# Queries and keys into even rows of the stripes by DMA from SBUF, and another order of the first batch

## The chip, the cores and the metric

The kernel runs on one core of a Trainium2 chip. The metric is the device time of one execution in microseconds (us), the median of several runs. Matrix products run on PE (TensorE; PEld is its weight load), reductions and elementwise work on DVE (VectorE), ACT (ScalarE) and POOL (GpSimd); SP (SyncE) issues nearly all DMAs, in the order of the program. An engine works through its own instructions in order, and a wait holds everything behind it on that engine.

## The reference

Eight sequences of 512 tokens with 256 channels, all in f32, go through four residual stages, each after a layer norm without gain:

```python
def attn_a(x, ...):                       # 16 heads of 16
    q = x @ Wq + bq
    kv = (x @ Wkv_down + bkv_down) @ Wkv_up + bkv_up      # 64 wide in between
    k, v = split(kv per head)
    q, k = rope(q), rope(k)
    att = q @ k.T / 4 + log_sparse + log(decay + 1e-9)    # depend on i - j alone
    out = softmax(att) @ v
    out = out + 0.2 * sigmoid(q @ mean(k).T) * mean(v)
    return out @ Wo + bo

def attn_b(x, ...):                       # one head, causal decay 0.96875, no softmax
    return ((x @ Wq.T + bq) @ (x @ Wk.T + bk).T * D) @ (x @ Wv.T)

x = x + attn_a(layernorm(x))
x = x + relu(layernorm(x) @ W1 + b1) @ W2 + b2
x = x + attn_b(layernorm(x))
x = x + relu(layernorm(x) @ W1 + b1) @ W2 + b2            # the same weights again
```

## The kernel before

The batch b is the outer index. In attention a, heads lie in stripes of 32 partitions, four heads to a group g, four groups to a batch: `qT[b % 2]` and `kT[b % 2]` are `[128, 4, 512]`, and head h of a group has rows 32h to 32h+31. In the kernel before, its 16 dimensions are rows 0 to 15 of the stripe. Row 16 of qT takes minus the row maximum (against a row of ones in kT), so that the product t comes out shifted. The rest of qT's stripe is zero and the rest of kT's is one.

One step of the main loop makes one score item: `s` (two heads, 128 queries by 512 keys, `score_item`), whose maximum DVE takes into `mr` (`reduce_item`). Eight items make a group. `shift(i)` turns the maxima, negates them on ACT and sends them by a DMA into qT (`neg`). Ten steps (`LAG`) after its `s`, the transposed product `t` is made (`prob_item`), ACT takes the exponential, DVE or POOL multiply with the decay `dec_a` (`soft_item`), and two steps later PE multiplies with the values (`pv_item`). The `s` items share two PSUM double banks with the later `t` items (`ps_sc`); the first `t` items and all other products share three banks (`ps_m`, `misc`).

All other work is cut into units (`Unit`), which stand in chains: front of a batch (layer norm `ln_units`, then `latent`, keys, queries, `values`, `gate`, `mean_v`, `through_wo`) and the rest of a batch (`wo_unit`, the two FFNs, attention b). A planner in Python (`step`, `issue`, and the loop at the end) goes through the steps with a model of the engines' clocks and puts units between steps where credit for PE time is left. `keep_in_program_order` pins the order that comes out.

A front makes queries and keys in half units: for e = 0, 1 (the two halves of a head's rotation) one product of PE, and two products of DVE with the tables of cosine and sine (`rc`, `rs`, six buffers of the tag `rot`). `turn(j)` sums them on POOL, writes the two results to a DRAM tile (`dk` or `dq`, by `[head, dimension, token]`), and reads this back into the stripes, four reads, one for each h:

```python
                move(d[:, e * HH : (e + 1) * HH, :], o)
            src = d.rearrange("(g s) r t -> s r g t", s=4)
            to = (qT, kT)[j][b % 2]
            for h in range(4):
                move(to[h * 32 : h * 32 + HD], src[h])
```

From the third batch on, another DMA puts zeros into the maxima's rows (`zero_rows`). `mean_k` and `gate` take the summed tiles for the gated memory; `mean_v` and `through_wo` make its other side (`mem`).

The first batch is written out by hand ahead of the loop: memsets of kT0 and qT0 on DVE, then statistics and norms, the bias products (`biases`, 32 products of one column), the weights' regrouping on ACT (`regroup`), transposes, `memory_buffers` (POOL memsets, small DMAs), then the first eight units of the front (latent, k0, k1, turn, mean_k, q0, q1, turn), then `late_loads` (dec_a, the second batch's x, wo, w1, w2, wvu, dec_b), `plain` and `product` (the combined weight of attention b's scores), values, gate and `mean_v`, `product_biases`, and the second pair of buffers on POOL (`buffers(1, gps)`). `through_wo` of the first batch waits in a chain for step 10.

Of the kernel before, what the change touches and what calls it, by code (L numbers as in the profile page):

```python
# [15 lines left out]
P = 128  # L16
B, T, D = 8, 512, 256
NH, HD = 16, 16
HH = 8
# [16 lines left out]
def tile_kernel(  # L36
# [44 lines left out]
    dr = ctx.enter_context(tc.tile_pool(name="dr", bufs=1, space=bass.MemoryType.DRAM))  # L81
# [8 lines left out]
    def move(to, src):  # L90
        tc.keep_in_program_order(nc.sync.dma_start(to, src))
# [11 lines left out]
    def keep(shape, name):  # L103
        return const.tile(shape, F32, tag=name, name=name)
# [26 lines left out]

    qT = [keep([P, NG, T], f"qT{i}") for i in range(2)]
# [7 lines left out]
    dq = [dr.tile([NH, HD, T], F32, tag=f"dq{i}", name=f"dq{i}") for i in range(2)]  # L140
    dk = [dr.tile([NH, HD, T], F32, tag=f"dk{i}", name=f"dk{i}") for i in range(2)]
# [11 lines left out]
    def buffers(i, eng):  # L153
        eng.memset(kT[i], 1.0)
        eng.memset(qT[i], 0.0)
        gps.memset(vaug[i], 1.0)

    def head_mask():
        dve.reduce_sum(hmask, ident.rearrange("p (h d) -> p h d", d=HH), axis=AX.X)
        gps.tensor_scalar(hmask, hmask, 0.5 / T, None, ALU.mult)  # L160
        gps.memset(kmean, 0.0)

    def memory_buffers():
        for i in range(2):
            gps.memset(gates[i], 0.0)
            move(gates[i][NH : NH + 1, :], rope[HD : HD + 1, 0, :])
            gps.memset(mem[i], 0.0)
        gps.memset(bo_row, 0.0)
        move(bo_row[NH : NH + 1, :], rows[D : 2 * D].unsqueeze(0))
        move(bvc, rows[0:D].rearrange("(c p) -> p c", p=P))  # L170
        gps.memset(vmean, 0.0)
        gps.memset(vmask, 0.0)
        gps.memset(vmask[:, :, NH : NH + 1], 1.0)
        for c in range(NC):
            dve.reduce_sum(
                vmask[:, c, c * HH : (c + 1) * HH], ident.rearrange("p (h d) -> p h d", d=HD), axis=AX.X
            )
        gps.tensor_scalar(bvc, bvc, 0.1, None, ALU.mult)

    late = {}  # L180

    def late_loads():
        late["dec_a"] = resident(decay_a, "dec_a")
        xs[1] = load_x(1)

        for g in range(NG):
            at_row = (g % 2) * 4 * HD
            move(wo_sb[at_row : at_row + 4 * HD, g // 2, :], wo.rearrange("(h d) g n -> h d g n", d=32)[:, :HD, g, :])
        late["w1"] = resident(w1, "w1_sb")
        late["w2"] = resident(w2, "w2_sb")  # L190

        move(wvu[:, :, :D], wb[:, :, 2, :])
        late["dec_b"] = resident(decay_b, "dec_b")
# [12 lines left out]

    wq_sb = keep([P, NC, 2, P], "wq_sb")
    wk_sb = keep([LAT, 2, P], "wk_sb")
    def regroup():
        for e in range(2):  # L210
            half_of = slice(e * HH, (e + 1) * HH)
            act.copy(wk_sb[:, e, :].rearrange("p (h d) -> p h d", d=HH), wk_in[:, :, half_of])
        for e in range(2):
            half_of = slice(e * HH, (e + 1) * HH)
            for c in range(NC):
                act.copy(wq_sb[:, c, e, :].rearrange("p (h d) -> p h d", d=HH), wq_in[:, c, :, half_of])
# [4 lines left out]
    def biases():  # L221
        pick = keep([P, 2, 32], "pick")
        for e in range(2):
            act.copy(
                pick[:, e, :].rearrange("p (s d) -> p s d", d=HH),
                ident.rearrange("p (s d) -> p s d", d=32)[:, :, e * HH : (e + 1) * HH],
            )
        ps = misc("qk_bias")
        for g in range(NG):
            for j, v in enumerate((V_BQ, V_BK)):  # L230
                for e in range(2):
                    mm(ps[g * 32 : g * 32 + 32, 2 * j + e : 2 * j + e + 1], pick[:, e, :], vec[:, v + g : v + g + 1])
        act.copy(qk_bias.rearrange("p j e -> p (j e)"), ps[:, :4])
# [12 lines left out]

    def plain(j):
        ps = misc(f"wr{j}")
        for o in range(NC):
            for c in range(NC):  # L250
                flip(ps[:, o * D + c * P : o * D + (c + 1) * P], wqk_in[:, c, j, o * P : (o + 1) * P])
        wr[j] = rs.tile([P, NC, D], F32, tag="xr", bufs=3, name=f"wr{j}")
        act.copy(wr[j].rearrange("p o d -> p (o d)"), ps)
# [83 lines left out]
    def front1(b):  # L337
        def latent():
            ps = misc(f"lat_{b}")
            for c in range(NC):  # L340
                mm(ps[:LAT, :], wd_sb[:, c, :], xT_a[b]["xT"][:, c, :], c == 0, c == NC - 1)
            lt = fr.tile([LAT, T], F32, tag="lat", name=f"lat_{b}")
            lsum[b] = fr.tile([LAT, 1], F32, tag="lsum", name=f"lsum_{b}")
            act.activation(lt, ps[:LAT, :], AF.Identity, bias=vec[:LAT, V_BD : V_BD + 1], accum_out=lsum[b])
            lat_a[b] = lt
# [15 lines left out]
        def mean_v():  # L361
            ps = misc(f"mv_{b}")
            for c in range(NC):
                mm(ps[:, c : c + 1], wv_sb[:, c * P : (c + 1) * P], lsum[b])
            m = fr.tile([P, NC], F32, tag="mv_a", name=f"mv_a_{b}")
            dve.scalar_tensor_tensor(m, ps[:, :NC], 0.1 / T, bvc, ALU.mult, ALU.add)
            for c in range(NC):
                gps.tensor_scalar(vmean[:, c, : NH + 1], vmask[:, c, :], m[:, c : c + 1], None, ALU.mult)
# [9 lines left out]
        u = {"lat": Unit(latent, 1720, (("ACT", 700),), after=[h0[2], h1[2]])}  # L378
# [11 lines left out]
    def front2(b, u1):  # L390
        rot = {}
        cos, nsin = rope_sb[:, 0, :], rope_sb[:, 1, :]

        def half_unit(j, e):
            ps = misc(f"{'qk'[j]}{e}_{b}")
            if j == 0:
                for c in range(NC):
                    mm(ps, wq_sb[:, c, e, :], xT_a[b]["xT"][:, c, :], c == 0, c == NC - 1)
            else:
                mm(ps, wk_sb[:, e, :], lat_a[b])  # L400
            for n, table in (("c", cos), ("s", nsin)):
                t = fr.tile([P, T], F32, tag="rot", bufs=6, name=f"r{n}{j}{e}_{b}")
                dve.scalar_tensor_tensor(t, ps, qk_bias[:, j, e : e + 1], table, ALU.add, ALU.mult)
                rot[n, e] = t

        def turn(j):

            d = (dq, dk)[j][b % 2]
            for e in range(2):
                o = rot["c", e]  # L410
                if e == 0:
                    gps.tensor_add(o, o, rot["s", 1])
                else:
                    gps.tensor_sub(o, o, rot["s", 0])
                move(d[:, e * HH : (e + 1) * HH, :], o)
            src = d.rearrange("(g s) r t -> s r g t", s=4)
            to = (qT, kT)[j][b % 2]
            for h in range(4):
                move(to[h * 32 : h * 32 + HD], src[h])
            if j == 0:  # L420
                if b > 1:
                    move(to[HD:P:32], zero_rows)
                rot["q"] = rot["c", 0], rot["c", 1]

        def mean_k():
            m = fr.tile([P, 2], F32, tag="mk", name=f"mk_{b}")
            for e in range(2):
                unused = fr.tile([P, T], F32, tag="unused", name=f"unused{e}_{b}")
                act.activation(unused, rot["c", e], AF.Identity, accum_out=m[:, e : e + 1])
                gps.tensor_scalar(kmean[:, e, :NH], hmask, m[:, e : e + 1], None, ALU.mult)  # L430

        def gate():
            ps = misc(f"ga_{b}")
            for e in range(2):
                mm(ps, kmean[:, e, :], rot["q"][e], e == 0, e == 1)
            act.activation(gates[b % 2][:NH, :], ps[:NH, :], AF.Tanh)
# [9 lines left out]
        ga = Unit(gate, 1720, (("ACT", 600),), after=[km, qt], needs=(("wo", b - 2),))  # L446
        return [lat] + k + [kt, km] + q + [qt, u1["v", 0], u1["v", 1], ga, u1["mv"], u1["me"]]
# [23 lines left out]
    def shift(i):  # L471
# [5 lines left out]
        act.dma_start(qT[b % 2][HD:P:32, g, :], neg)  # L477
# [237 lines left out]
    order0 = front2(0, front[0][1])  # L715
    (n0, n1), u0 = (front[0][0][:3], front[0][0][3:]), front[0][1]
    buffers(0, dve)
    head_mask()
    n0[0].fn(), n1[0].fn()
    biases()  # L720
    regroup()
    n0[1].fn(), n1[1].fn()
    n0[2].fn(), n1[2].fn()
    memory_buffers()
    for u in order0[:8]:
        u.fn()
    late_loads()
    plain(0), plain(1)
    for u in order0[8:12]:
        u.fn()  # L730
    product(), product_biases()
    buffers(1, gps)


# [127 lines left out]
    for u in front[0][0] + order0[:12]:  # L862
        u.done = 0
    order0[12].step = 10
    chains = [order0[12:], setup]
# [168 lines left out]
```

## Time and profile before

| what | us |
|---|---|
| median of 3 runs | 1354.7 |
| lowest, highest | 1354.05, 1356.53 |
| the profiled execution's own time | 1355.33 |
| its span in the profile | 1353.5 |
| PE busy in the span | 1278.4 (94%) |
| DVE, ACT, POOL busy | 805.8, 450.8, 408.3 |
| first score product `s` starts | 39.31 |
| first `t` product starts | 65.37 |

The profile is of one execution. Its times count from the start of the span. An entry of a timeline gives start, length, engine, line, operation, tile written, tiles read, shapes and the number of instructions merged into it, and in brackets how long the engine stood idle before and what ended that. L198, L201, L69 and L91 are the helpers `mm`, `flip`, `Engine` and `move`, so one goes by the tiles' names. A product in f32 appears as two matmul records. "PEclk" is the granted TensorE clock, as a share of full speed in the windows and in tenths in the page's row.

### The profile page before, as it was taken

What the parts mean: (1) busy time and instruction counts of PE and PEld (TensorE: products, weight loads), DVE (VectorE), ACT (ScalarE), POOL (GpSimd) and SP (SyncE); (2) the same over time, 40 slices, a digit from 0 to 9 for tenths busy, and PEclk for the clock granted to TensorE, in tenths of its full rate; (3) what the DMA queues carried; (4) which work ended last, traced back from release to release, by engine and by line L of the source; (5) the groups of instructions that cost most, each with busy time, mean ns of one, the idle gap of its engine ahead of it and who ended that gap; (6) DMA issues with size and microseconds to landing.
All of it is one profiled execution on the core that took longest, in us unless ns stands there. A gap on an engine that the chain in (4) does not pass through costs nothing. (4 is left out here: it accounts for less than half of the span.)

```text
span 1353.5 us, 15551 instructions
## 1 busy us (share of the span) xinstructions
PE 1278.4 (94%) x6116; PEld 632.2 (47%) x6116; DVE 805.8 (60%) x1323; ACT 450.8 (33%) x646; POOL 408.3 (30%) x461
## 2 busy tenths in 40 slices
PE   7889998999899998999999999999999999999989
PEld 3323233535354553545544454535444554455665
DVE  4577976678656686546765667646755484433120
ACT  2034434342434324333343323342343233331201
POOL 4165443233422323223331414213321232222010
PEclk9689989999999999999999999999999999999999
DMA  4440040003000210004000300003000000000000
GB/s 122 134 79 1 1 79 1 1 16 64 1 1 1 63 33 1 0 5 91 1 1 1 68 28 1 1 1 79 1 1 0 17 1 1 1 16 1 0 16 16
DMA packets 22159, 32.09 MB, mean 24 GB/s; under 512 B 2987, under 2 KB 12652, under 8 KB 21806
## 3 DMA queue, kind: packets, MB, share of 16 engines
q1 hardware_dynamic: 21446, 30.83, 10.2%
q8 instruction: 48, 0.79, 0.3%
q10 hardware_dynamic: 640, 0.26, 0.1%
q14 instruction: 25, 0.20, 0.0%
HBM read 18.24 MB, written 12.58 MB: 23 GB/s over the span
## 5 line engine op out<-in xcount | busy, mean ns | idle before, releaser
L69 DVE TENSOR_REDUCE mr<-s 128x2 f32<-128x1024 f32 x256 | 312.4, 1221 | 274.9 <-PE t L198 264.5
L69 ACT ACTIVATE p<-t 128x1024 f32<-128x1024 f32 (+1 forms) x290 | 264.0, 924 | 554.4 <-PE t L198 496.1
L69 POOL TENSOR_TENSOR p<-p,dec_a 128x512 f32<-128x512 f32 x182 | 233.1, 1302 | 490.0 <-ACT p L69 435.6
L198 PE MATMUL s<-kT,qT 32*128 32x512 f32 x1024 | 297.6, 664 | 40.3 <-DVE mr L69 36.5
L198 PE MATMUL t<-qT,kT 32*128 32x512 f32 x1024 | 297.0, 647 | 4.8 <-DVE mr L69 2.5
L69 DVE TENSOR_TENSOR p<-p,dec_a 128x512 f32<-128x512 f32 x330 | 230.1, 738 | 21.5 <-ACT p L69 21.3
L198 PE MATMUL x<-w_sb,h_x 128*128 128x256 f32 x1024 | 233.1, 383 | 0.0
L198 PEld LDWEIGHTS x<-w_sb,h_x 128*128 128x128 f32 x1024 | 190.7, 190 | 52.5 <-issue 27.6
L198 PEld LDWEIGHTS s<-kT,qT 32*128 32x128 f32 x1024 | 81.1, 189 | 208.1 <-DVE mr L69 85.2
L198 PE MATMUL pv<-p,va 128*32 128x512 f32 x1024 | 152.2, 614 | 3.7 <-DVE p L69 3.1
L69 ACT ACTIVATE h_x<-hx,vec 128x512 f32<-128x512 f32 x128 | 88.0, 688 | 156.3 <-PE hx L198 156.3
L198 PE MATMUL hx<-xT_g,w_sb 128*128 128x512 f32 x256 | 122.1, 622 | 0.7 <-ACT xT_g L69 0.7
L198 PE MATMUL hx<-xT_f,w_sb 128*128 128x512 f32 x256 | 119.0, 604 | 0.0
L69 DVE TENSOR_TENSOR x<-x,x 128x256 f32<-128x256 f32 x64 | 27.1, 424 | 153.9 <-PE x L198 153.8
L198 PEld LDWEIGHTS t<-qT,kT 32*128 32x128 f32 x1024 | 80.4, 184 | 22.0 <-issue 9.1
L198 PEld LDWEIGHTS hx<-xT_g,w_sb 128*128 128x128 f32 x256 | 48.0, 196 | 67.7 <-issue 59.8
L198 PEld LDWEIGHTS hx<-xT_f,w_sb 128*128 128x128 f32 x256 | 46.2, 192 | 57.5 <-issue 54.3
L198 PEld LDWEIGHTS pv<-p,va 128*32 128x32 f32 x1024 | 23.6, 108 | 78.2 <-issue 35.4
L69 POOL TENSOR_TENSOR x<-x,row 128x256 f32<-128x256 f32 x64 | 47.7, 765 | 38.4 <-DVE xn_g L69 20.4
L69 POOL TENSOR_TENSOR rc<-rc,rs 128x512 f32<-128x512 f32 x32 | 42.6, 1354 | 10.9 <-DVE rs L69 10.9
L198 PE MATMUL bs<-xT_r,ret 128*128 128x512 f32 (+3 forms) x128 | 38.3, 442 | 0.4 <-DVE mv_a L69 0.4
L198 PE MATMUL bo<-ret 128*128 128x256 f32 x160 | 36.7, 382 | 0.0
(130 smaller groups left out, 1034.5 us busy)
## 6 DMA issues: line engine op xcount, KB each, us to landing
dk<-rc SPq DMA_DIRECT2D x16, 256.0 KB
kT<-dk SPq DMA_DIRECT2D x32, 128.0 KB
dq<-rc SPq DMA_DIRECT2D x16, 256.0 KB
qT<-dq SPq DMA_DIRECT2D x32, 128.0 KB
out_dram<-x SPq DMA_DIRECT2D x32, 128.0 KB
x<-in_x_dram SPq DMA_DIRECT2D x7, 512.0 KB
w_sb<-in_w_dram SPq DMA_DIRECT2D x2, 1024.0 KB
x<-in_x_dram SPq DMA_DIRECT2D x2, 256.0 KB
```

Source lines behind the costliest of these rows:

```text
L69: ins = f(*a, **k)
L198: tc.keep_in_program_order(nc.tensor.matmul(o, lhsT=l, rhs=r, start=start, stop=stop))
```

## The change

- The two DRAM tiles are gone. `stripes(j, g, e)` sends 32 partitions of a summed tile (group g, half e, 2 KB in each) straight into the stripes of qT or kT: half e = 0 goes to rows 0, 4, 8, ... and e = 1 to rows 2, 6, 10, ... So the dimensions lie in the even rows, and the maxima's row is now row 1 of the stripe. A batch has 16 such DMAs in place of 4 writes and 8 reads.
- The first batch gets another order. PE starts with 14 products of the identity with itself (`warm`), whose result nobody reads. The latent of the first batch is made in two halves of 256 tokens, each after its transposes, so that `lsum` has two columns and `mean_v` twice the products. Regrouping is split. Memsets of kT1, qT1 and va1 come earlier, and qT0's comes after the norms. q0 comes ahead of the keys, q1 after them, with its two products in a tile of the tag `p`; the sums of q1 and q0 run on DVE.
- SP gets x_1, dec_a, the gates' rows and bvc ahead of the stripes; the 16 stripes then go group by group; the other late loads follow.
- values, `plain` and `product` stand after the stripes' issue and ahead of the loop; gate, `product_biases`, `mean_v` and `through_wo` (now from step 4) go into the loop as a chain. `wr` lies in the buffer of the tag `x1`.

```diff
-    dq = [dr.tile([NH, HD, T], F32, tag=f"dq{i}", name=f"dq{i}") for i in range(2)]
-    dk = [dr.tile([NH, HD, T], F32, tag=f"dk{i}", name=f"dk{i}") for i in range(2)]
...
+    def loads_before_scores():
+        xs[1] = load_x(1)
+        late["dec_a"] = resident(decay_a, "dec_a")
+        for i in range(2):
+            move(gates[i][NH : NH + 1, :], rope[HD : HD + 1, 0, :])
+        move(bvc, rows[0:D].rearrange("(c p) -> p c", p=P))
+
     def late_loads():
-        late["dec_a"] = resident(decay_a, "dec_a")
-        xs[1] = load_x(1)
+        move(bo_row[NH : NH + 1, :], rows[D : 2 * D].unsqueeze(0))
...
+    def warm(n):
+        ps = misc("warm")
+        for j in range(n):
+            mm(ps[:, j % 4 * P : (j % 4 + 1) * P], ident, ident)
...
-        def latent():
-            ps = misc(f"lat_{b}")
+        def latent(part=0, parts=1):
+            if part == 0:
+                lat_a[b] = fr.tile([LAT, T], F32, tag="lat", name=f"lat_{b}")
+                lsum[b] = fr.tile([LAT, parts], F32, tag="lsum", bufs=1, name=f"lsum_{b}")
+            ps = misc(f"lat_{b}_{part}")
+            n = T // parts
+            cols = slice(part * n, (part + 1) * n)
...
-        def half_unit(j, e):
+        def half_unit(j, e, order="cs"):
...
+                if b == 0 and (j, e) == (0, 1):
+                    if not spare:
+                        spare["t"] = at.tile([P, 2, T], F32, tag="p", bufs=4, name="rq1_0")
+                    t = spare["t"][:, "cs".index(n), :]
+                else:
+                    t = fr.tile([P, T], F32, tag="rot", bufs=6, name=f"r{n}{j}{e}_{b}")
...
+        def rotate(j, e, eng):
+            o = rot["c", j, e]
+            if e == 0:
+                eng.tensor_add(o, o, rot["s", j, 1])
+            else:
+                eng.tensor_sub(o, o, rot["s", j, 0])
+            rot[j, e] = o
+
+        def stripes(j, g, e):
+            move((qT, kT)[j][b % 2][2 * e : P : 4, g, :], rot[j, e][g * 32 : g * 32 + 32, :])
+
         def turn(j):
-            d = (dq, dk)[j][b % 2]
             for e in range(2):
...
-                move(d[:, e * HH : (e + 1) * HH, :], o)
-            src = d.rearrange("(g s) r t -> s r g t", s=4)
-            to = (qT, kT)[j][b % 2]
-            for h in range(4):
-                move(to[h * 32 : h * 32 + HD], src[h])
-            if j == 0:
-                if b > 1:
-                    move(to[HD:P:32], zero_rows)
-                rot["q"] = rot["c", 0], rot["c", 1]
+                rotate(j, e, gps)
+                for g in range(NG):
+                    stripes(j, g, e)
+            if j == 0 and b > 1:
+                move(qT[b % 2][1:P:32], zero_rows)
...
-        act.dma_start(qT[b % 2][HD:P:32, g, :], neg)
+        act.dma_start(qT[b % 2][1:P:32, g, :], neg)
...
-    buffers(0, dve)
-    head_mask()
+    dve.memset(kT[0], 1.0)
+    gps.memset(vaug[0], 1.0)
+    memory_buffers()
+    picks()
+    warm(14)
+    regroup_k()
     n0[0].fn(), n1[0].fn()
+    n0[1].fn(), n1[1].fn()
+    n0[2].fn()
     biases()
-    regroup()
-    n0[1].fn(), n1[1].fn()
-    n0[2].fn(), n1[2].fn()
-    memory_buffers()
-    for u in order0[:8]:
-        u.fn()
+    regroup_q(0)
+    latent(0, 2)
+    masks()
+    dve.memset(qT[0], 0.0)
+    gps.memset(kT[1], 1.0)
+    gps.memset(qT[1], 0.0)
+    gps.memset(vaug[1], 1.0)
+    loads_before_scores()
+    n1[2].fn()
+    latent(1, 2)
+    regroup_q(1)
+    half_unit(0, 0)
+    half_unit(1, 0), half_unit(1, 1, "sc")
+    rotate(1, 0, gps), rotate(1, 1, gps)
+    half_unit(0, 1, "sc")
+    rotate(0, 1, dve), rotate(0, 0, dve)
+
+    for g in range(NG):
+        for j, e in ((1, 0), (1, 1), (0, 1), (0, 0)):
+            stripes(j, g, e)
     late_loads()
-    plain(0), plain(1)
-    for u in order0[8:12]:
-        u.fn()
-    product(), product_biases()
-    buffers(1, gps)
+    order0[1].fn(), order0[2].fn()
+    plain(0), plain(1), product()
+    gps.tensor_scalar(bvc, bvc, 0.1, None, ALU.mult)
+    order0[0].fn()
...
-    for u in front[0][0] + order0[:12]:
+    km0, _, _, ga0, mv0, me0 = order0
+    for u in front[0][0] + [front[0][1]["lat"], km0]:
         u.done = 0
-    order0[12].step = 10
-    chains = [order0[12:], setup]
+    ga0.after = []
+    me0.step = 4
+    chains = [[ga0, Unit(product_biases, 2400, (("DVE", 500),)), mv0, me0], setup]
```

## The prediction

> **What bounds the kernel now.** I read the page first, then windows over the first 110 us, then the timelines of PE, SP and DVE there, then the waits.
>
> ```profile
> span 1353.5 us, 15551 instructions
> PE 1278.4 (94%) x6116; PEld 632.2 (47%) x6116; DVE 805.8 (60%) x1323; ACT 450.8 (33%) x646; POOL 408.3 (30%) x461
> PEclk9689989999999999999999999999999999999999
> ```
>
> PE is busy 94% of the span, so work taken off other engines in the middle is worth little. What stands out is the second and third digit of the clock row. Finer windows (columns: stretch, length, busy PE, PEld, DVE, ACT, POOL, granted clock, DMA share, GB/s):
>
> ```profile
> 34.00:37.00 3.00, 2.29 (x21) 2.20 (x19) 1.40 (x4) 0.00 (x0) 3.00 (x3) 1.00 0.07 24
> 37.00:39.30 2.30, 0.00 (x0) 0.02 (x1) 0.85 (x1) 0.00 (x0) 0.82 (x1) 0.85 0.96 160
> 45.00:50.00 5.00, 5.00 (x14) 1.51 (x12) 4.05 (x7) 0.00 (x0) 0.95 (x2) 0.50 1.02 280
> 50.00:55.00 5.00, 5.00 (x16) 1.89 (x16) 4.60 (x7) 0.56 (x1) 0.00 (x0) 0.50 0.57 224
> 65.00:70.00 5.00, 5.00 (x23) 1.83 (x23) 3.47 (x5) 2.30 (x5) 2.49 (x2) 1.00 0.00 0
> ```
>
> PE stands from 36.3 to 39.3 and the clock falls to 0.50 (the 1-us window 38:39 reads 0.81, so at 38.6). It returns in the window 62:64 (0.87, so at 62.5). Now the PE timeline:
>
> ```profile
> 12.32 3.67 PE L198 MATMUL lat<-xT_a,wd_sb 128*64 128x512 f32 x4 [0.68 <-ACT xT_a L69]
> 16.86 3.78 PE L198 MATMUL k<-lat,wk_sb 64*128 64x512 f32 x4 [0.87 <-ACT lat L69]
> 20.56 5.87 PE L198 MATMUL q<-xT_a,wq_sb 128*128 128x512 f32 x8
> 39.31 14.04 PE L198 MATMUL s<-kT,qT 32*128 32x512 f32 x28 [3.02 <-DMA qT<-dq]
> 63.50 1.93 PE L198 MATMUL lat<-xT_a,wd_sb 128*64 128x512 f32 x4 [0.68 <-ACT xT_a L69]
> 65.37 0.70 PE L198 MATMUL t<-qT,kT 32*128 32x512 f32 x2
> 66.43 1.98 PE L198 MATMUL k<-lat,wk_sb 64*128 64x512 f32 x4
> ```
>
> The same lat and k products take 3.67 and 3.78 in the first batch and 1.93 and 1.98 in the second. So PE also ran at half speed up to about 25 us, though the clock row says 1.00 there. The first seven score steps take 14.04 us, 2.0 each. Why the scores start so late is in SP's timeline:
>
> ```profile
> 23.46 1.77 SPq L91 DMA_DIRECT2D dk<-rc  x2
> 27.68 1.75 SPq L91 DMA_DIRECT2D kT<-dk  x4
> 29.53 1.55 SPq L91 DMA_DIRECT2D dq<-rc  x2
> 36.13 1.72 SPq L91 DMA_DIRECT2D qT<-dq  x4
> ```
>
> Queries leave for DRAM at 29.5 and are read back only at 36.1. In the waits of PE this DMA appears once (3.0 us, one time): later batches never wait for it.
>
> **The change part by part.** My marker is the first t product, at 65.4 us. Behind it the same steps are planned, and PE stays the limit. So I sum up to the marker, against this execution (span 1353.5, time 1355.33; the median 1354.7 is 0.6 below it).
>
> *Front, at full PE speed.* 14 products of ident run from about 1.4 us, when ident is ready: 28 records. A 128-column record at half speed is about 0.21 (0.85, the half-speed pace of 512 columns, divided by four), so at most 6 us, until 7.4. They delay nothing: x_0 is summed to 512 KB by 3.8 us, and transposes began at 7.75. Dropping qT's memset (1.76) and hmask (0.23) from ahead of the statistics lets these start at about 3.8 instead of 5.18. On POOL the moved memsets (2.5 us at 8.2, plus kmean 0.3) now stand ahead of ve_a; they end at about 5.1, when ve_a could have started at 4.8, so 0.3 lost. First norm at 6.15 (was 7.29); the second one took 2.37 beside those memsets and should take 0.73.
>
> Then: transposes 6.6 to 7.3; xT copy 0.59 beside 32 bias products (1.1); lat half 8.4 to 9.4; second transposes to 9.9; ACT's lat and copy to 10.7; lat half to 11.7; q0 (four of eight records at 0.48) to 13.7; k0, k1 to 15.6; q1 to 17.5. DVE makes 8 rotation products (0.66 apart) from 13.8 to 19.1 and two sums until 20.5. POOL makes k's sums (2.49) from about 17.2. ACT's regroup_k waits for wk_in (there by 6.06) and regroup_q for wq_in (there at 8.16, wanted at 8.6): hidden; a later wq_in would hold lat, queued behind it on ACT, one for one. The memsets of kT1, qT1, va1 (4.7 us on POOL) go to about 8 to 13, ahead of k's sums at 17: free.
>
> *Stripes.* A new DMA, SBUF to SBUF, 32 rows of 2 KB. The trace has no such row. From below: neg, 8 KB SBUF to SBUF, is issued in 0.54. From above: qT<-dq, 128 KB, landed about 2.7 after its issue on a full queue. I take 0.42 to issue (kT<-dk's) and 2.5 to land; the four of group 0 are out at 20.9 and landed by 23.5 (bounds 22.5 and 25). The other twelve issue until 26 and are wanted one group per 8 steps.
>
> The Trainium skill, "DMA: Bandwidth & Descriptors", section "Rules for kernel authors", speaks against this: many small transfers should be coalesced, since under 64 KB overhead is most of the cost; its fixed part is about 2 us. Were the 16 to follow each other at that price, group 1 would land at 18 + 8 x 2.1 = 35, still before its step 8 (about 40). By the rule or by the 0.42, the sum is the same.
>
> *Filling the wait.* v (2.0), plain (1.0), product (2.0), already there, run from 17.5; with bank waits for DVE's va (1.62 after the sums) they end at about 24.5. That, not the DMA, starts the scores: 24.5, against 39.3. Some twenty handoffs at under 0.1 us add 1.5: 26.
>
> *Scores to marker.* It took 26.1. At full speed PE needs 10 steps x 1.05, transposes 0.9, mx 0.3, me 1.1, lat 1.9: 14.7. DVE needs 10 x 1.23, layer norm 3.3: 15.6. Moved in: gate 2.0, product_biases 2.4, mean_v with a second column 1.1, and DVE's 1.5 (wvu's row took 1.32 beside POOL). PE 20.2, DVE 17.1; they partly wait for each other through two score banks, so 22. Marker at 48: 17.4 saved.
>
> Here a rule and the trace differ. The skill's "TensorE: Matmul & The Clock Gate", "Part 1", says one busy window of about 3.4 us brings full speed back and one idle window takes it. The changes I can place (38.6, 62.5, 93.2, 103.5, 171.8) are indeed whole multiples of 3.41 apart. But score products alone, with PE shown busy 5.00 of 5, did not bring it back for 23.9 us. By the rule the half-speed stretch would cost some 2 us in scores and the gain be about 12; by the trace it costs what I counted.
>
> *Loads.* x_1, dec_a, gates' rows and bvc (6 issues, some 2.2 us of SP) move ahead of the stripes, into 7 to 9 us, and lengthen the stream of loads from 12.2 to about 15.3; all that the front needs stands ahead of them. wo, now behind the 16 stripes, lands at about 31, wanted by me at about 33; without that cover PE stands 1 to 3 us. w1, w2, wvu, dec_b are wanted far later.
>
> *Later batches.* Per batch SP issues 16 stripes (6.7 us) instead of 4 at 0.55 and 8 at 0.42 (5.6), without its waits for dk and dq. Nothing behind them on SP (x two batches on, outputs) is near: kT and qT of batch 1 landed by 99 and its scores start at about 134. I count zero. The order of units behind the marker may shift by a few steps; half-speed stretches such as 93.2 to 103.5 (worth some 4 us) may come or go: plus or minus 5.
>
> **The rivals.**
> 1. *Clock stays half in part* (27%). For: between 7 and 12 PE holds only short pieces, and the window before 93.2, with 1.1 us of work, was enough to lose the clock; scores alone did not regain it. Against: gate, me, transposes and lat are mixed in. Scores at 33, or 26 plus 30 us: marker 55 to 60, gain 5 to 10: about 1347.
> 2. *More comes free* (10%): the front as summed without slack, and the stall at 90.7 to 93.0 goes too: gain 25, 1329.
> 3. *Stripes are slow in every batch* (4%), the other side. All four of one group read the same 32 partitions. q's eight start at 90 and scores want them at 134: it decides from 5.6 us apiece, one after another. At 6 each, a batch waits 4 us and the lost clock costs 4 more: seven times 8 less 17 gives 1394. Against: 128 KB reads were issued 0.42 apart.
> 4. *Given back* (4%): a new order of units loses as much behind the marker as was won: 1354. That the change does not do what it says I exclude: the order is pinned by hand.
>
> **How the numbers follow.** Likeliest (55%): 1355.3 - 17.4 - 0.6 = 1337. Range 1327 to 1350: rival 2 below, rival 1 above, with the 5 us of order; outside are rivals 3, 4 and the edges. Faster by over 0.2% (2.7 us, about what this measurement can tell from no change) in the likeliest, 1 and 2: 0.92; same 0.04 (rival 4); slower 0.04 (rival 3).
>
> **What would show it.** lat and k at about half of 3.67 and 3.78; first s near 26 without a wait for DMA; no 0.50 between 30 and 55; first t near 48; stripes issued about 0.42 apart; tail unchanged. Wrong, if lat halves take 1.8 each, if the clock reads 0.50 in the scores, or if s of batch 1 waits for DMA.

## The result, and the profile after

The changed kernel takes 1343.06 us (median of 4 runs, 1340.52 to 1343.37) against 1355.15 for the kernel before on the same chip: a ratio of 0.9906 [0.9889, 0.9923]. So it is faster by about 12 us. The forecast was 1337, with a gain of 17.4. The result lies inside the forecast's range, 1327 to 1350, on the side of its first rival.

The profiled execution took 1343.3. The page of the changed kernel (its span, the busy times, the clock row):

```profile
span 1341.5 us, 15714 instructions
PE 1274.7 (95%) x6152; PEld 634.4 (47%) x6152; DVE 804.2 (60%) x1325; ACT 450.8 (34%) x648; POOL 405.3 (30%) x459
PEclk9689999999999999999999999999999999998999
```

PE's busy time fell by 3.7 us only, for a span that is 12.0 shorter. That does not make the rest time in which PE stood: the busy time now holds the 5.2 us of `warm`, which fill time in which PE stood before. Without them PE's work is 8.9 us shorter, and only the other 3.1 of the 12.0 are time in which PE stood. The second digit of the clock row is still 6, so a half-speed stretch is still there. The page's DMA traffic fell from 32.09 MB to 23.70 MB with the trips through DRAM gone.

PE's timeline of the changed kernel:

```profile
1.34 5.17 PE L193 MATMUL warm<-ident 128*128 128x128 f32 x28 [1.34 <-POOL ident masks.py:199]
7.94 1.08 PE L193 MATMUL lat<-xT_a,wd_sb 128*64 128x256 f32 x4
...
11.10 1.08 PE L193 MATMUL lat<-xT_a,wd_sb 128*64 128x256 f32 x4 [1.50 <-ACT xT_a L69]
12.10 1.98 PE L193 MATMUL q<-xT_a,wq_sb 128*128 128x512 f32 x4
14.02 1.98 PE L193 MATMUL k<-lat,wk_sb 64*128 64x512 f32 x4
...
24.35 1.13 PE L193 MATMUL s<-kT,qT 32*128 32x512 f32 x4
25.41 1.12 PE L193 MATMUL ga<-rc,kmean 128*128 128x512 f32 x2
27.23 1.84 PE L193 MATMUL bb<-vec,wr 128*128 128x1 f32 x16
28.93 0.59 PE L193 MATMUL bb<-both,ones 128*128 128x1 f32 x4
29.45 1.13 PE L193 MATMUL s<-kT,qT 32*128 32x512 f32 x4
30.50 1.05 PE L193 MATMUL mv<-lsum,wv_sb 64*128 64x1 f32 x8
...
34.00 2.08 PE L193 MATMUL s<-kT,qT 32*128 32x512 f32 x4 [0.49 <-DVE mr L69]
...
37.50 1.19 PE L193 MATMUL me<-wo_sb,vmean 128*128 128x256 f32 x2 [0.27 <-DMA wo_sb<-in_wo_dram]
...
48.81 1.22 PE L193 MATMUL t<-qT,kT 32*128 32x512 f32 x2
...
54.76 1.98 PE L193 MATMUL k<-lat,wk_sb 64*128 64x512 f32 x4
```

The front runs at full speed: the two lat halves sum to 2.16 where lat took 3.67, and k takes 1.98 where it took 3.78. The first s starts at 24.35 with no wait in brackets (39.31 before, behind a wait of 3.02 for qT). Up to 31 four s records take 1.13. At 34.00 four take 2.08: the clock has gone. It is back by 54.76, where k takes 1.98. The windows show the same (columns: stretch, length, busy PE, PEld, DVE, ACT, POOL, granted clock, DMA share, GB/s):

```profile
26.00:29.00 3.00, 3.00 (x21) 2.28 (x19) 0.82 (x2) 0.59 (x1) 0.00 (x0) 1.00 0.40 106
29.00:32.40 3.40, 3.40 (x23) 2.29 (x24) 2.11 (x5) 0.00 (x0) 0.00 (x0) 1.00 0.30 78
32.40:36.00 3.60, 3.11 (x10) 0.50 (x4) 2.68 (x6) 0.00 (x0) 1.62 (x4) 0.50 0.42 136
46.06:49.48 3.42, 3.42 (x12) 1.42 (x14) 2.32 (x4) 0.63 (x2) 0.00 (x0) 0.50 0.01 2
50.00:55.00 5.00, 5.00 (x21) 1.30 (x14) 1.36 (x2) 1.95 (x5) 2.49 (x2) 0.71 0.01 3
```

The clock is at half speed from 32.4 to 52.9. That is 20.5 us, six times 3.41; before it was seven times 3.41 (38.6 to 62.5). Two lines deserve notice. In the second, the 3.40 us just before the loss, PE is shown busy for all 3.40. In the fourth, PE is busy for all of one such stretch of 3.42, and the clock still does not come back at its end.

The lead of the changed kernel over the one before, taken as the difference of the starts of the same instruction:

| instruction | before | after | lead |
|---|---|---|---|
| first s | 39.31 | 24.35 | 15.0 |
| first t | 65.37 | 48.81 | 16.6 |
| k of the second batch | 66.43 | 54.76 | 11.7 |
| end of span | 1353.5 | 1341.5 | 12.0 |

The order around the marker changed, so the starts need care. Before, lat of the second batch stands ahead of the first t; after, it stands behind (50.82, 2.94 us long), so the first t flatters. k is too harsh: after, one step more (an s and a t, 48.81 to 50.82, so 2.0 us) stands ahead of it. Either way, with lat added to the first t or the step taken off k, the lead for equal work is about 13.7. Behind k it moves between 10.7 and 14.9 (read at the products mx, which turn the score maxima, group by group), and ends at 12.0. So of the 15.0 won at the first s, 1.3 were lost up to the marker and 1.7 behind it. The forecast had counted on 4.1 more between the first s and the marker (13.3 to 17.4); that did not come.

### The profile page after: what moved, and what is told of

Same layout as the page of the kernel before. It is cut to its first block, busy times and chain, and to the rows that moved or that the text cites. A ratio compares the mean times of both kernels' runs of the same rounds, so it can differ in the third digit from the quotient of the medians.

```text
span 1341.5 us, 15714 instructions
## 1 busy us (share of the span) xinstructions
PE 1274.7 (95%) x6152; PEld 634.4 (47%) x6152; DVE 804.2 (60%) x1325; ACT 450.8 (34%) x648; POOL 405.3 (30%) x459
## 2 busy tenths in 40 slices
DMA packets 18576, 23.70 MB, mean 18 GB/s; under 512 B 3500, under 2 KB 13165, under 8 KB 18223
## 5 line engine op out<-in xcount | busy, mean ns | idle before, releaser
L193 PE MATMUL s<-kT,qT 32*128 32x512 f32 x1024 | 293.1, 660 | 38.6 <-DVE mr L69 37.8
L193 PE MATMUL hx<-xT_f,w_sb 128*128 128x512 f32 x256 | 121.9, 617 | 0.0
L69 POOL TENSOR_TENSOR rc<-rc,rs 128x512 f32<-128x512 f32 x30 | 39.6, 1340 | 5.0 <-DVE rs L69 5.0
```

Source lines behind the costliest of these rows:

```text
L69: ins = f(*a, **k)
L193: tc.keep_in_program_order(nc.tensor.matmul(o, lhsT=l, rhs=r, start=start, stop=stop))
```

## The experiments

Two theories were set against each other. One: the score stage is slow because the clock falls, and the clock falls with what TensorE's array has to do, not with how long PE is shown busy. The other: the stage is held by something else (two score banks that wait for DVE, a late wo), and the clock only follows. In all kernels here that carry an added "fill" product, its result is overwritten by the score product that follows; "warm" products have no reader. No output changes by them. Ratios are against the kernel before; a lead is a lead over it in the profiled executions, and these are single ones. Where the work ahead of k differs between two that are compared, the text says so.

**Fill products beside the scores** (on top of the change):

```diff
+            if s < LAG:
+                mms.append((ps[:, 0, :256], ident, rope_sb[:, 0, :256]))
```

> The changed kernel with one more product in each of the first ten score steps (identity times 256 columns of the rope table, written where the step's own score product then starts anew, so nothing of the result changes). Theory A: the score stage of the changed kernel loses about 8 us because score products alone are too little activity for the clock, which falls to 0.50 at 32.4; the fill keeps it at 1.00 up to the first t product, each fill costs 0.43 us, and k of the second batch starts at 48 to 50 instead of 54.8; about 1337 us. Rival B: the stage is bound by waits (two score banks, DVE's maxima, wo's DMA) and the clock costs nothing there; then ten fills come on top, k starts at 57 to 59, about 1347 us.

1348.41 (20 runs, 1340.25 to 1356.92), ratio 0.9965 [0.9947, 0.9983]: worse than the change alone. The clock was lost at 29.7, before the fills had had a chance. PE's timeline and a window of this kernel:

```profile
26.92 1.84 PE L193 MATMUL bb<-vec,wr 128*128 128x1 f32 x16
...
42.00:46.00 4.00, 4.00 (x12) 2.04 (x10) 2.28 (x4) 0.00 (x0) 0.00 (x0) 0.50 0.04 18
```

The 3.41 us ahead of 29.7 hold mostly `bb`, the one-column products of product_biases (1.84, then 0.58). PE had no gap in them. Then fills and scores ran at half speed until 46.8. So the fills did not hold the clock in this execution, which speaks against the first theory as it was stated; but it was one-column products that lost it, and a fill costs 0.6 at full speed and 1.22 at half.

**The front's warm products taken out** (on top of the change):

```diff
-    warm(14)
```

> The changed kernel without the 14 products of the identity at the start. If these set PE's speed in the front: lat halves take 1.8 instead of 1.08, q and k 3.7 instead of 1.98, the first score starts at 30 to 32 instead of 24.4, and the time is about 1349 us. Rival: PE comes up to speed by itself or the front is bound by x, ACT and DVE; first score at 25 to 26, time within 1.5 us of the changed kernel's 1343.

1346.36, ratio 0.9936 [0.9918, 0.9954]. PE's timeline of this kernel:

```profile
8.66 1.97 PE L193 MATMUL lat<-xT_a,wd_sb 128*64 128x256 f32 x4
...
14.24 3.53 PE L193 MATMUL q<-xT_a,wq_sb 128*128 128x512 f32 x4
```

Without them the lat halves take 1.97 in place of 1.08 and q 3.53 in place of 1.98; the first s starts at 28.04, so `warm` is worth 3.7 us there and 2.6 at k (57.40). Its score stage was at half speed for three windows (34.5 to 44.7), not six. The two intervals of the whole time overlap, so how much of this survives is not settled.

**The stripes alone** (the kernel before, its order kept, the two DRAM tiles replaced by the 16 stripes):

```diff
-                move(d[:, e * HH : (e + 1) * HH, :], o)
...
-                move(to[h * 32 : h * 32 + HD], src[h])
+                for g in range(NG):
+                    stripes(j, g, e)
```

> The kernel before with the stripes alone (no DRAM tiles, even rows, maxima in row 1), first batch in its old order. Expected: stripes of group 0 land by about 34, so the first score starts when PE is through with product_biases, at 36.3 instead of 39.3; PE does not stand, so the clock holds for one or two windows of 3.4 us and then falls in the score stage: 1350 to 1352 us. Rival: the stripes also pay in every later batch (a wait for DRAM that the profile does not show), 1340 to 1345; other rival: 16 small DMAs are slower in later batches, above 1355.

1352.13, ratio 0.9984 [0.9967, 1.0]. PE's timeline and two windows of this kernel:

```profile
34.68 1.14 PE L195 MATMUL s<-kT,qT 32*128 32x512 f32 x8
...
34.00:37.00 3.00, 1.82 (x15) 0.98 (x14) 2.18 (x3) 0.00 (x0) 2.29 (x2) 0.99 0.73 223
37.00:42.00 5.00, 4.01 (x10) 1.51 (x12) 4.15 (x8) 0.00 (x0) 0.95 (x2) 0.50 0.92 248
```

The wait for qT is gone and the first s comes 4.6 us earlier, yet the clock falls at 36.95 and stays down for 23.9 us, exactly as long as before. The stand of 3 us was not needed to lose it; a wait of 1.31 us for DVE stood in the window ahead of the loss. What was won at the first s is what is left at the end (lead 4.7 at k, 4.1 at the end of the profiled run; 2.5 in the medians).

**The new order alone** (the changed kernel, with queries and keys through the DRAM tiles):

```diff
-    for g in range(NG):
-        for j, e in ((1, 0), (1, 1), (0, 1), (0, 0)):
-            stripes(j, g, e)
+    for j, e in ((1, 0), (1, 1), (0, 1), (0, 0)):
+        leave(j, e)
+    back(1), back(0)
```

> The changed kernel's order of the first batch with queries and keys still going through DRAM tiles (rows 0 to 15 of the stripes, maxima in row 16, as before). Expected: the round trip of about 8.8 us from the last sum (30.5 to 39.3 in the kernel before) puts the first score at 29 to 31; PE stands from 24.4, the clock falls to 0.50 there and returns only with the first t products; about 1349 to 1351 us. Rival: values, plain and product hide the round trip, first score at 25, 1343 us.

1354.31, ratio 0.9992 [0.9978, 1.0006]: no difference. PE's timeline and a window of this kernel:

```profile
30.97 3.12 PE L197 MATMUL s<-kT,qT 32*128 32x512 f32 x4 [7.13 <-DMA qT<-dq]
...
24.00:28.00 4.00, 0.00 (x0) 0.00 (x0) 0.57 (x1) 0.00 (x0) 0.00 (x0) 0.74 0.70 126
```

All that the new order wins in the front PE spends waiting, 7.13 us, for the trip through DRAM. The clock falls in that wait, at 25.9, and stays down for nine windows, to 56.6; the gate, bias and mean products moved into this stage run at half speed too. The stripes alone bring about 2.5 us, the order alone nothing that can be told, both together 12. The two parts need each other: the order ends sooner only if the keys and queries arrive, and their arrival counts only if PE has got that far.

**product_biases out of the score stage:**

```diff
-    me0.step = 4
-    chains = [[ga0, Unit(product_biases, 2400, (("DVE", 500),)), mv0, me0], setup]
+    pb = Unit(product_biases, 2400, (("DVE", 500),), step=LAG + 1)
+    chains = [[ga0, pb, mv0, me0], setup]
```

> The changed kernel with product_biases, mean_v and through_wo of the first batch held until score step 11, when t products run too; gate stays. Theory A (28 products of one column in the score stage leave PE nearly without activity for a window of the clock): the clock holds 1.00 from the front to the t products; s, gate, transposes and lat up to k of the second batch take about 23 us from 24.4, k starts at 47 to 49 instead of 54.8, and the time is about 1337 us. Rival B (score products alone, two of them at a time on 32 rows each, are too little activity): the clock still falls, at 33 to 37, k starts at 53 to 55, 1342 to 1344 us.

> The same with one product of the identity with 256 columns of the rope table in each of the first ten score steps, overwritten by the step's own score product. Theory A: the clock held anyway, the fills add up to 10 x 0.43 us of PE, of which some hides beside DVE's maxima; k at 49 to 52, 1338 to 1341 us. Rival B: the fills are what holds the clock; k at 49 to 52 where the kernel without them has 53 to 55, so 3 us faster than that one.

The second one has the fills besides. In the chain, mean_v and through_wo stand behind product_biases and move with it. Without fills: 1348.63, ratio 0.9951 [0.9936, 0.9965]. With fills: 1346.74, 0.994 [0.9922, 0.9957]. PE's timeline and a window of the one without fills, then a line of PE's timeline and three windows of the one with:

```profile
34.04 3.20 PE L193 MATMUL s<-kT,qT 32*128 32x512 f32 x8 [0.74 <-DVE mr L69]
...
32.00:36.00 4.00, 3.20 (x10) 1.30 (x12) 3.11 (x6) 0.00 (x0) 0.94 (x2) 0.62 0.28 74
```

```profile
49.01 1.02 PE L193 MATMUL bb<-both,ones 128*128 128x1 f32 x4 [1.49 <-POOL ones L69]
...
36.00:42.00 6.00, 6.00 (x27) 2.49 (x25) 5.17 (x9) 0.82 (x2) 0.94 (x2) 1.00 0.84 345
44.00:48.00 4.00, 3.52 (x25) 2.46 (x24) 1.86 (x3) 1.67 (x3) 1.68 (x2) 1.00 0.02 4
48.00:52.00 4.00, 2.99 (x13) 2.96 (x14) 0.48 (x3) 0.00 (x0) 0.95 (x2) 0.60 0.00 0
```

Score products with short waits for DVE lose the clock, at 32.9 (1.31 us of waiting in the 3.41 before). The same score products with a full-array fill of 256 columns in each step keep it, at 1.00 through the whole stage. It is then lost at 48.8, in the block of one-column products that now stands behind the stage; PE also waits in it, 1.49 us for `ones`, so this loss is not the products' alone. From the first product of the stage to the first t it is 21.3 us without fills and 20.3 with: the fills add PE work, and the stage becomes shorter. This speaks for the first theory against the second.

**Only product_biases late, with no fill, a half fill and a full fill.** The chain is now `[ga0, mv0, me0, pb]`, with `pb` at step `2 * LAG + 2`.

> The changed kernel with product_biases alone held until step 22, where s, t and pv products surround it; mean_v and through_wo stay early; no fill. If score products alone cannot hold the clock, it falls to 0.50 between 30 and 37 as before and t starts near 47; k near 53 because 2 to 4 us of one-column products are gone from the half-speed stretch, of which some 2 come back at step 22: about 1342 us. If the one-column products alone were to blame, the clock holds, k at 46 to 48 and 1337 us.

> The same with a fill product of 128 columns in each of the first ten score steps (full array, 0.21 us at full speed). If this much activity holds the clock: ten steps of 1.4 us, gate, mean_v, through_wo and transposes, first t at 43 to 45, k at 47 to 49, 1338 us. If it is too little, the clock falls as without fill and ten fills at half speed cost 4 us on top of it: k at 57, 1346 us.

> The same with fills of 256 columns, which held the clock up to the block of one-column products before. Expected: clock at 1.00 from the front to k of the second batch, first t at 45 to 46.5, k at 49 to 51 instead of 54.8 in the changed kernel; product_biases at step 22 costs 2 us there: about 1339 to 1340 us, 3 us faster than the changed kernel. Rival: the stage is bound by waits and the fills only add, 1345 or more.

The medians are 1346.11, 1353.88 and 1357.37; the ratios 0.9947 [0.9926, 0.9967], 0.9981 [0.9969, 0.9993] and 1.0017 [1.0001, 1.0033]. More fill was worse, against what the first theory would have it do. The profiled execution with the full fill, 1353.01, is the fastest of its twelve; the one without fill, 1351.88, the slowest of its seven. PE's timeline of the one with the full fill, and a window:

```profile
34.14 0.67 PE L193 MATMUL me<-wo_sb,vmean 128*128 128x256 f32 x2 [0.94 <-DMA wo_sb<-in_wo_dram]
...
35.97 0.92 PE L193 MATMUL me<-wo_sb,vmean 128*128 128x256 f32 x2 [1.16 <-DMA wo_sb<-in_wo_dram]
...
34.00:37.00 3.00, 1.70 (x5) 1.24 (x6) 0.54 (x2) 0.00 (x0) 0.00 (x0) 0.88 1.02 354
```

A new wait had taken the place of the old cause. With product_biases gone, PE comes to `me` before wo has landed; it stands for 0.94 and 1.16, and the clock is lost at 36.3, for seven windows, in which the fills take twice their price. The kernel with no fill waits for wo too, 1.33 and 0.76 us, but it had lost the clock before that, at 31.8, behind a wait of 1.31 for DVE; it is at half speed until 55.7. The wait for wo is the one that the forecast priced for a lost cover (1 to 3 us). The changed kernel itself waits for wo only 0.27.

**wo ahead of the stripes, with and without fills.** The four loads of wo move from `late_loads` into `loads_before_scores`; the chain is that of the runs just told.

> The kernel with fills of 256 columns and product_biases at step 22, with one more edit: the four loads of wo go out ahead of the stripes (beside x_1 and dec_a), not behind them. If the two waits for wo (0.94 and 1.16 us) were what lost the clock at 36, it now holds from the front to k of the second batch: through_wo without a wait, first t at 45 to 47, k at 48.5 to 50.5, time 1338 to 1341 us. Rival (fills of this size do not hold the clock, the run in which they did was a matter of where its windows fell): the clock falls between 30 and 37 again, k at 60 to 63, 1350 us or more.

> The same without fills. If score products alone are too little activity, the clock falls between 30 and 37 though PE waits for no DMA: first t at 47 to 50, k at 52 to 54, 1342 to 1345 us. If the waits for wo and the block of one-column products were all, the clock holds, k at 45 to 47, and this is the fastest version at about 1335 us.

With fills: 1343.47, ratio 0.9913 [0.9881, 0.9944]. Without: 1342.64, 0.9916 [0.9891, 0.9941]. PE's timeline of the one with fills, then of the one without, then windows of the one with:

```profile
23.36 0.59 PE L193 MATMUL s<-rope_sb,ident 128*128 128x256 f32 x2
...
32.89 1.13 PE L193 MATMUL me<-wo_sb,vmean 128*128 128x256 f32 x4
...
45.55 0.70 PE L193 MATMUL t<-qT,kT 32*128 32x512 f32 x2
...
49.54 1.98 PE L193 MATMUL k<-lat,wk_sb 64*128 64x512 f32 x4
...
92.36 1.95 PE L193 MATMUL bb<-vec,wr 128*128 128x1 f32 x16 [0.20 <-ACT p L69]
```

```profile
25.02 1.17 PE L193 MATMUL s<-kT,qT 32*128 32x512 f32 x4
...
31.47 1.62 PE L193 MATMUL s<-kT,qT 32*128 32x512 f32 x4 [1.32 <-DVE mr L69]
...
54.31 1.98 PE L193 MATMUL k<-lat,wk_sb 64*128 64x512 f32 x4
```

```profile
34.00:38.00 4.00, 4.00 (x17) 1.49 (x17) 2.99 (x6) 0.00 (x0) 0.00 (x0) 1.00 0.99 413
42.00:46.00 4.00, 4.00 (x21) 1.68 (x19) 3.24 (x5) 0.85 (x2) 0.15 (x1) 1.00 0.02 4
...
92.00:96.00 4.00, 3.23 (x26) 3.00 (x28) 2.80 (x7) 0.79 (x2) 0.71 (x2) 0.78 0.00 0
96.00:100.00 4.00, 4.00 (x20) 0.83 (x24) 1.46 (x3) 1.09 (x2) 1.31 (x2) 0.50 0.00 0
```

With wo there and the fills in, the clock stays at 1.00 from the front to k, and k starts at 49.54: a lead of 16.9 over the kernel before, 5.2 more than the change has. Of these, 2.2 are product_biases, which this kernel has still to do. Without fills and with the same loads the clock is lost at 32.0, with PE waiting for DVE (1.32) and for no DMA, and k starts at 54.31. From the first fill (23.36), or without fills from the first s (25.02), to k it is 26.2 and 29.3 us: the fills make the stage 3.1 us shorter, although they themselves take 6.6 us of PE. That is the cleanest pair of the study: same order, same loads, the only difference is work whose result nobody reads. It is one profiled execution of each, though, and the one without fills had lost the clock once more, from 21.7 to 25.1, ahead of the stage.

But the lead did not last. At 92.36 product_biases, postponed, stands in one block, the clock goes from 94.2 to 101, and the lead drops from 16.3 to 11.2 over those groups (3.4 of that is the block itself, from 92.36 to the next score product); it ends at 9.3 in the profiled run. In the medians the two kernels are alike.

**product_biases in five parts** (on top of the one with fills and wo early; two products each, one part per two steps):

```diff
+    pb = [Unit(lambda k=k: bias_part(k), 500, (("DVE", 250),), step=2 * LAG + 3 + 2 * k) for k in range(5)]
+    chains = [[ga0, mv0, me0] + pb, setup]
```

> The kernel with fills and early wo, with product_biases cut into five units of two products, two steps apart from step 23 on, instead of one block of 20 products at step 22. If the block was what gave back 5 us between the second and the third group's maxima (clock lost from 94 to 102), the parts cost about 2.5 us at full speed and no clock: the lead over the kernel before, 16 us at the second group's maxima, ends at 13 to 14.5, and the time is 1339 to 1341 us, some 2 to 3 us faster than the changed kernel. Rival (the clock goes there anyway, from the stall of t behind va near 75): no gain, 1343 to 1345 us.

1342.15 (4 runs, 1340.78 to 1344.42), ratio 0.9893 [0.9872, 0.9913]. A window of this kernel where the block had stood:

```profile
96.00:100.00 4.00, 3.13 (x25) 1.89 (x25) 3.63 (x6) 2.38 (x5) 0.98 (x2) 1.00 0.01 2
```

The first two parts lie in this window (96.1 and 99.2), the last starts at 113.9. Spread between other work, the same products did not lose the clock in this execution: it stays at 1.00 from 84.3 to 155.9. That the spreading did it is not shown. Of the five kernels with the block at step 22, three lost the clock in it (those without fill and the one with fills and wo early), and two kept it (the half fill and the full fill with wo late, where the block stands from 103 to 106). The score stage held the clock too: first s at 27.38, k at 52.89, and from the first fill to k 26.0 us, as in the run before. But this execution lost the clock once in its front, from 12.6 to 16.0, and came to its first s 3.5 us later than the run before. The time can't be told from that of the changed kernel: the intervals overlap. So no version here clearly beats the change.

**The clock over all executions.** The profile shows one execution of each kernel, but the mean granted clock is on record for every one. The clock has only the values 1.00 and 0.50 in these traces, so the time at half speed can be worked out from it. For product_biases, mean_v and through_wo behind the stage it was 64.5 to 72.9 us without fills (16 executions) and 45.7 to 56.4 with them (9): no overlap. With wo early it was 61 on average without fills and 51 with them (4 each), and 48 with the parts. So the fills do win clock, and not in one execution only. They do not win time over the changed kernel, which has 61. In the 20 executions of the first fill kernel the time goes with the clock: one took 1340.25 at 0.985, ten took 1345.15 to 1348.50 at 0.977 to 0.979, nine took 1354.03 to 1356.92 at 0.969 to 0.972. Between the means of the last two groups that is 8 us for 18 us at half speed. By an estimate from this, the 10 us less at half speed are worth about 4.5 us, and the fills cost up to 6.6 of PE.

## Why the prediction was right, and where its size was off

**The front** was right in mechanism and 1.7 us too cautious. The first s starts at 24.35; 26 was forecast. lat, k and q run at full speed as summed. One named risk came in part: wq_in landed late, ACT's copy was held by it, and lat behind that copy by 1.50 us. ACT's timeline of the changed kernel:

```profile
9.62 0.50 ACT L69 COPY wq_sb<-wq_in 128x128 f32<-128x128 f32 x2 [1.41 <-DMA wq_in<-in_wq_dram]
```

What made up for it was the fill of the wait. SP has finished the first group's stripes by about 22, and PE reaches the scores at 24.35 without the slack of 1.5.

**The stripes** were right in what they do and half too low in price. SP's timeline of the changed kernel, in the first batch and in a later one:

```profile
18.96 1.72 SPq L90 DMA_DIRECT2D kT<-rc  x2
20.77 0.54 SPq L90 DMA_DIRECT2D qT<-rq  x1
21.41 0.54 SPq L90 DMA_DIRECT2D qT<-rc  x1
...
30.89 2.42 SPq L90 DMA_DIRECT2D wo_sb<-in_wo_dram  x4
...
63.01 4.98 SPq L90 DMA_DIRECT2D kT<-rc  x8
```

Each takes SP 0.54 to 0.62, not 0.42; a batch's 16 keep SP for about 9.9 us, where 6.7 were counted. It costs nothing: PE waits for no such DMA in any batch. In the first batch it pushes wo back: the first of its loads is issued at 30.9, and `me` waits 0.27 at 37.5, where landing at 31 was counted. The rule on small transfers, quoted in the forecast, speaks of less than 64 KB; these have just 64 KB, so the runs do not test it. What they show is that 16 of them in a row cost PE no wait.

**Scores to marker** is the term that was mis-sized. It was given 22 us, lat included, for PE at full speed. It took 24.46 to the first t (24.35 to 48.81), and 27.4 with lat's 2.94: 5.4 more than forecast, and no less than the 26.1 of the kernel before, now with the gate, bias and mean products moved in. The balance: 17.4 forecast, plus 1.7 in the front, minus 5.4 in this stage, is a lead of 13.7 at the marker; minus 1.7 behind it, 12.0. That the first t came at 48.81, where 48 was forecast, is no hit: lat was missing ahead of it. What failed is the assumption that a stage with "gate, me, transposes and lat" mixed in keeps the clock: the forecast itself had named a clock of 0.50 in the scores as a sign of being wrong, and there it was. Two of the other pieces mixed in, bb and mv, are one-column products; they fill some 1.4 us of the 3.4 ahead of the loss here, and bb alone 2.2 of the 3.4 in the first fill kernel. With the clock held, the sum for this term was about right: with fills and wo early the stage up to lat's end takes 24.6 us from the first s, of which 6.0 are fills, and lacks 2.2 of bb, so an estimate is 20.8 for the forecast's 22.

That the cause is the clock and not the two score banks is shown by the pair with wo early: with the clock held, 26.2 us (6.6 of them fills) and without, 29.3; the parts, with the clock held, repeat it with 26.0. That PE's busy time does not decide is shown by windows in which PE is busy throughout: the clock was lost behind one here (3.40 of 3.40) and behind one in the first fill kernel, and it did not come back behind one at 49.5. The window of the parts held it with PE busy 3.13 of 4. That it is the array's work which decides fits all of this, but is argued: in the kernels without fill of the two pairs PE also stood for 1.3 us ahead of the loss, and the fills fill that time. This was rival 1's mechanism: it was given 27%, a gain of 5 to 10 and 1347; the time lies between it and the likeliest case. Its 27% was too low, since the trace of before already showed scores alone failing to win the clock back for 23.9 us. That the total still came within 6 us of the forecast is in part luck: the front, better by 1.7, covered some of the 5.4.

**Later batches at zero** held within its margin: a lead of 13.7 at the marker, 12.0 at the end. The order of units and single half-speed stretches move it by up to 3 us between, inside the 5 allowed. Rivals 2, 3 and 4 did not happen: the gain is 12 and not 25, PE's wait for stripes is nil, and what was given back is 1.7 of 13.7.

**Rule and trace.** The Trainium skill's "TensorE: Matmul & The Clock Gate", "Part 1", has one busy window restore the speed. With "busy" read as PE's busy time, the changed kernel contradicts it (PE busy for all of 46.06 to 49.48, at half speed before and after); with it read as enough work in the array, it can agree. By the rule the forecast's sum was a gain of about 12, the size that was measured, but not for its reason: the sum had the half-speed stretch of the kernel before cost little, and what happened is that the stretch came again, six windows of it.

Open are: how much work in a window is enough (neither an edge nor a unit for it can be read from these runs); whether score products without any wait would hold the clock; and whether the clock can be held at a price below what it wins, since the fills, on all executions, cost about what they won.

## What to carry to other kernels

Read the granted clock beside each stage before you price it, and ask what the array does there, not how busy PE is shown: products with few rows or one column can leave TensorE at half speed while its row reads 9. Check what they did to the clock before counting PE time at full speed; spreading them between wide ones is worth a try, but was not shown to help by itself. Work that is added to hold the clock costs PE time of its own: judge it by the whole kernel over several executions, not by the stage in one. Where a wait is removed, the next load in the queue is then wanted earlier; move it too, or the new wait may cost the clock again.

## What the runs showed of the hardware that was not expected

- Full-array products with no use can shorten a stage: 20 records of 256 columns, 6.6 us of PE, made it 3.1 us shorter (29.3 to 26.2). Where they failed to hold the clock they lengthened it, at 1.22 us a pair in place of 0.6.
- The clock changes at steps 3.41 us apart in every trace, but where those steps fall differs from run to run. With the same front order as in the changed kernel, where it held, the profiled runs with product_biases late (step `LAG + 1`, without fill), with the half fill, and in five parts lost the clock between 12 and 17 (q 3.22 to 3.61 in place of 1.98). In these three, lat had waited 1.92 to 2.39 us for the copy xT_a; in the eight other kernels with this front and `warm`, at most 1.50. Two others, both without fill, lost it at 21 to 25 (ct 3.59 and 3.68 in place of 1.99). One kernel's times spread with the share of the clock that it was granted: 1340.25 at 0.985 to 1356.92 at 0.970 over 20 runs of the first fill kernel. What sets where the steps fall was not tested.
- A DMA from SBUF to SBUF of 32 rows of 2 KB (64 KB) occupies SP for 0.54 to 0.62 us, longer than the 0.42 of the 128 KB read from DRAM that it replaced.
